# Products made ahead and output rows held back in a graph layer whose edge sums run for most of the kernel

## The chip, the cores and the metric

The kernel runs on one core of a Trainium2 chip. The metric is the device time of one execution in microseconds (us). Three runs of the kernel before took 307.3, 313.0 and 314.23 us, so its median is 313.0 us. One execution was recorded by the hardware profiler; all durations below are of that execution.

The engines are TensorE (PE, with its weight loads shown as PEld), VectorE (DVE), ScalarE (ACT), GpSimd (POOL) and SyncE (SP), which issues most transfers. Each works through its own instructions in order. Transfers run on 16 DMA engines that all queues share.

## The reference

A graph layer over 12,500 nodes of 128 numbers and 412,500 edges of 48 numbers. The edges are sorted by the node they end in (`dst`). `batch0` is all zeros, so one row of the globals serves every node.

```python
h = relu(layernorm(x))
agg = segment_sum(edge_attr, dst, 12500)          # 12500 x 48
z = concat([h, agg, globals[0]]) @ W1 + b1        # 240 -> 256
out = x + relu(z) @ W2 + b2                       # 256 -> 128
```

All of it is in float32.

## The kernel before

**Edge sums.** Edges come in chunks of 896 (seven per partition). A step takes eight chunks, so there are 58 steps (`NS`), of some 217 nodes each. For a step, VectorE builds a one-hot matrix of each edge's place in a window of 32 nodes (`onehot`, L294), TensorE multiplies it with the edges into tile `ps` (`aggregate`), and ScalarE copies the result to `sums` (`keep_sums`, L340). Two steps later TensorE places the sums with a second one-hot (`place_columns`, `place`, tile `pp`), and VectorE adds them (`add`, L371) into `aggT`, which holds the transposed sums: one column per node, 112 of 128 partitions. In a step of TensorE's order the placing of an earlier step comes first, then pieces of the node work, then the aggregation of the step itself. `aggT` is set to zero on POOL in 16 parts of 797 columns (`zero`), each some steps before the sums reach it.

**Node work.** The nodes are in 26 blocks: block 0 has 212 nodes, blocks 1 to 23 have 512, and the last two 256. For a block, in this order: load of its rows (`load_x`, SP, L378), statistics on DVE (`stats`), the root on ACT (`root`), factors on DVE, x + b2 on POOL (`plus_b2`, L411, tile `xb`), normalisation with ReLU on ACT (`normal`, L418, tile `xn`), four transposes on TensorE (`turn`, L182, tile `pt`), a copy out of PSUM (`keep`, L432, tile `hT`), two products with the upper part of W1 into PSUM (`first_h`, tile `ph`), the products with the sums added in the same PSUM tile (`first_a`), bias and ReLU (`relu`, L475), the products with W2 (`second`, tile `po`), the addition of `xb` (`result`, L489, tile `ot`) and the store (`store`, L497, on POOL except for the last two blocks, which SP stores).

**What sets the order.** The order of the whole program is written out. `at(k, f, ...)` puts an operation in half-step `k` (two half-steps to a step). `ready[j]` is the last step whose sums can touch block `j`; `piece` places the turning, the products, and so on of the blocks one after another, where an estimate of TensorE's time per half-step still has room. From that estimate the loop over the steps also chooses how many pairs of edge chunks are multiplied together (`twos`: fewer instructions, more time each).

**Loads.** SP issues the edges of step `s + 3` during step `s`, four transfers of 336 KB a step. `few` lets a load wait until one of the five before it has landed, and in the loop also for the last TensorE instruction that stands before it:

```python
if len(flight) == FLIGHT:
    tc.add_manual_dep(now.ins, flight.pop(0).ins.name, LANDED, reason="few loads under way")
flight.append(now)
if paced:
    tc.add_manual_dep(now.ins, last[0], LANDED, reason="in TensorE's pace")
```

Block rows wait in a pool of five buffers (`xp`), so a load of x also waits until the block five before it has been normalised and added to b2. `xb` has four buffers, so `plus_b2` of a block waits for the result of the block four before it. The weights are eight transfers issued by POOL at the start (`load_weights`). Two extra products of ones (`spare`) stand in half-steps 1 and 3, two more stand before the loop; nothing reads them.

Every matmul goes through one helper line (L178, transposes L182), so tiles tell them apart in the profile. A float32 matmul appears as two records, a transpose as one.

Of the kernel before, what the change touches and what calls it, by code (L numbers as in the profile page):

```python
# [8 lines left out]
F32 = mybir.dt.float32  # L9
I32 = mybir.dt.int32  # L10
AF = mybir.ActivationFunctionType
OP = mybir.AluOpType
# [5 lines left out]
P = 128  # L18
# [4 lines left out]
def kernel(  # L23
# [12 lines left out]
    nc = tc.nc  # L36
    N, D = x.shape
# [59 lines left out]
    ready = [max(s for s in range(NS) if low(s) - BEFORE < a + m * r) for a, m, r in blocks]  # L97


    parts = [(0, 4 * CS)]  # L100
    while parts[-1][0] + parts[-1][1] < NCH:
        c0 = parts[-1][0] + parts[-1][1]
# [38 lines left out]
    with fast:  # L141
# [224 lines left out]
        def add(s):  # L366
            _, v = nc.values_load_multi_w_load_instructions(
                at_i[0:1, s:s + 1], engines=[DVE], min_val=low(s), max_val=high(s),
                skip_runtime_bounds_check_because="clamped to these on the chip")
            to = aggT[:, ds(v[0], WG)]  # L370
            nc.vector.tensor_tensor(to, to, banks_p.pop(s)[:HI + DE, :WG], OP.add)  # L371

        def load_x(j):
            a, m, r = blocks[j]
            xt = xp.tile([P, 4, D], F32, name="xt")
            xv = xt.rearrange("p r d -> p (r d)")[:, :r * D]
            for p0, p1 in by_rows(m):
                now = nc.sync.dma_start(xv[p0:p1], rows_of(x, a + p0 * r, p1 - p0, r))  # L378
            if j > 1:
                few(now)  # L380
            xs[j] = xt

# [24 lines left out]

        def plus_b2(j):
            a, m, r = blocks[j]
            xb = mp.tile([P, 4, D], F32, name="xb", bufs=4)  # L410
# [37 lines left out]
        def first_h(j, h):  # L448
            n, small, ph = bank(j, h)
            product(ph, w1h[:, h * P:(h + 1) * P], ht[j][:, :n], start=(h == 0 or not small),  # L450
                             stop=False, skip_group_check=True)
            hids[j, h] = ph

        def first_a(j):
            a, m, r = blocks[j]
            n = m * r
            for q in range(0, n, 256):
                w = min(256, n - q)  # L460
                for h in range(NH):
                    c = BEFORE + a + q
                    k = slice(0, DE) if bank_is_shared(j) else slice(HI * h, HI * h + DE)
                    product(hids[j, h][:, q:q + w], w1a[k, h * P:(h + 1) * P], aggT[k, c:c + w],
                                     start=False, stop=True, skip_group_check=True)

        def relu(j):
            a, m, r = blocks[j]
# [16 lines left out]

        def result(j):
            a, m, r = blocks[j]
            ot = mp.tile([P, 4, D], F32, name="ot", bufs=3)
            nc.vector.tensor_tensor(ot[:m, :r], pos_o[j][:m, :r], xbs[j][:m, :r], OP.add)  # L489
            outs[j] = ot  # L490

# [6 lines left out]

        def load_weights():
            nc.gpsimd.dma_start(w1h, W1[0:D])  # L500
            nc.gpsimd.dma_start(w1a[0:DE], W1[D:D + DE])
# [56 lines left out]
        with tc.manual_schedule():  # L558
# [14 lines left out]
            ZN = 16  # L573
            zw = -(-aggT.shape[1] // ZN)


            def clear_tail():
                nc.gpsimd.memset(etail, 0.0)
                nc.gpsimd.memset(relt, -1.0)

            def zero(i):
                nc.gpsimd.memset(aggT[:, i * zw:min((i + 1) * zw, aggT.shape[1])], 0.0)

            zero(0)
            nc.vector.memset(eps, EPS)
# [37 lines left out]
            onehot(0)  # L623
            onehot(1)
            load_weights()
# [27 lines left out]
            piece.last = 0  # L653


            def behind(name, j):
                return where[name, j] // 2 * 2 + 2

            def turned(j):
                k = 8 + 3 * j if j < 2 else 2 * placed(ready[j]) - 2  # L660
                piece("turn", j, k, 0.16 * blocks[j][2], (turn, (j,)), (keep, (j,)))

            def hidden_x(j):
                us = 0.22 * blocks[j][2]
                piece("h0", j, behind("turn", j), us, (first_h, (j, 0)))
                piece("h1", j, where["h0", j], us, (first_h, (j, 1)))
# [2 lines left out]
            hidden_x(0)  # L669
            for j in range(NW):  # L670
                r = blocks[j][2]
                piece("a", j, 2 * placed(ready[j]) + (4 if j == 0 else 2), 0.27 * r, (first_a, (j,)), (relu, (j,)))
                if j + 1 < NW:
                    turned(j + 1)
                for q in range(0, r, 2) if j + 1 < NW else ():
                    piece("o", j, behind("a", j), 0.9, (second, (j, q)))
                if j + 1 < NW:
                    hidden_x(j + 1)
                    at(where["o", j] + 1, result, j)
                    at(where["o", j] + 1, store, j)  # L680
# [3 lines left out]
            for j in range(NBL):  # L684
                k = where["turn", j]
                if j > 1:
                    at(k - 17, load_x, j)
                near = j < 2
                at(k - (6 if near else 8), stats, j)
                at(k - (4 if near else 6), root, j)  # L690
# [6 lines left out]
            taken = {where["turn", j] for j in range(NBL)}  # L697

            def apart(k, f, *a):
                while k - 1 in taken or k in taken or k + 1 in taken:  # L700
# [2 lines left out]
                at(k, f, *a)  # L703
                return k

            at(0, shift_dst, 1)
            at(2, spread_dst, 1, 0)
            at(2, spread_dst, 1, 1)
            at(2, middles, 0)
            at(4, own_and_ref, 1)  # L710
            at(6, middles, 1)
# [241 lines left out]
```

## Time and profile before

| | |
|---|---|
| runs | 307.3, 313.0, 314.23 us; median 313.0 |
| profiled execution | 310.81 us, of which 309.1 are its span (first to last instruction) |
| PE busy | 291.4 us (94%) |
| PEld busy | 227.5 us (74%) |
| DVE busy | 231.8 us (75%) |
| ACT busy | 164.1 us (53%) |
| POOL busy | 78.5 us (25%) |
| moved by DMA | 95.15 MB, 308 GB/s over the span |
| granted TensorE clock | 0.994 on average |

The share of the clock is what the throttle granted. The start of an aggregation is the first weight load into `ps` of a step. By the timeline, step 0 begins at 8.76 us, step 1 at 14.97, step 7 at 45.79, step 8 at 51.10, step 15 at 86.24, step 30 at 159.70, step 50 at 258.94 and the last, 57, at 293.24 us. Stretches of idle TensorE say where it waits, and the waits of SP say whether the loads wait for transfers to land or for TensorE.

### The profile page before, as it was taken

The page shows a single profiled execution, that of the slowest core. Times are in us where ns is not written, and L with a number is a line of the kernel's source. Part 1 is how long each engine was busy: PE and PEld are TensorE (multiplying, and loading weights), DVE is VectorE, ACT ScalarE, POOL GpSimd, SP SyncE. Part 2 cuts the span into 40 slices and gives each one's busy share as a digit, 9 for nine tenths or more (in the row PEclk, how much of TensorE's full clock was granted, in tenths as well). Part 3 has the DMA queues.
Part 4 walks back from the last instruction along what each step waited for, and adds up shares of the span by engine and source line. Part 5 has one row for each costly group of instructions (what it writes and reads, how often), then busy time and mean ns, then how long its engine had stood idle before and what let it go on. Part 6 is the DMA issues. An engine that isn't in the chain of part 4 may idle for free. (4 is left out here: it accounts for less than half of the span.)

```text
span 309.1 us, 14799 instructions
## 1 busy us (share of the span) xinstructions
PE 291.4 (94%) x6397; PEld 227.5 (74%) x6398; DVE 231.8 (75%) x530; ACT 164.1 (53%) x426; POOL 78.5 (25%) x87
## 2 busy tenths in 40 slices
PE   7888999999999999989999999999999899999982
PEld 3577767767877877866877887876887777786772
DVE  6867958987695967759976598779984899797221
ACT  2223696465564764645454487655452884665320
POOL 8221041032120544222134204123303033223000
PEclk9997999999999999999999999999999999999999
DMA  7999999999999999999999999999999999998102
GB/s 231 313 322 316 338 338 336 343 361 296 336 344 333 365 349 331 312 333 287 319 354 326 363 335 333 346 348 322 315 367 312 289 354 321 375 357 279 39 0 75
DMA packets 69717, 95.15 MB, mean 308 GB/s; under 512 B 5018, under 2 KB 64611, under 8 KB 69647
## 3 DMA queue, kind: packets, MB, share of 16 engines
q1 hardware_dynamic: 67439, 87.53, 85.3%
q0 software_dynamic: 2208, 6.63, 5.6%
q8 instruction: 51, 0.84, 1.1%
q14 instruction: 19, 0.16, 0.1%
HBM read 87.74 MB, written 6.40 MB: 305 GB/s over the span
## 5 line engine op out<-in xcount | busy, mean ns | idle before, releaser
L178 PE MATMUL ps<-e,oh 128*32 128x48 f32 (+1 forms) x5288 | 117.6, 218 | 7.2 <-issue 4.6
L178 PEld LDWEIGHTS ps<-e,oh 128*32 128x32 f32 (+1 forms) x5288 | 100.7, 116 | 31.4 <-issue 10.2
L294 DVE TENSOR_TENSOR oh<-iota,rel 128x1792 f32<-128x1792 f32 (+1 forms) x60 | 116.0, 1936 | 0.0
L340 ACT COPY sums<-ps 128x192 f32<-128x192 f32 (+1 forms) x165 | 43.1, 262 | 97.5 <-PE ps L178 94.9
L497 POOL DMA_DIRECT2D out_dram<-ot x25 | 14.0, 560 | 207.9 <-DVE ot L489 156.1
L371 DVE TENSOR_TENSOR aggT<-aggT,pp 112x246 f32 x58 | 23.7, 409 | 39.6 <-PE pp L178 30.3
L411 POOL TENSOR_TENSOR xb<-xt,b_sb 128x512 f32<-128x512 f32 (+2 forms) x26 | 46.5, 1792 | 15.3 <-DMA xt<-in_x_dram 9.8
L178 PE MATMUL po<-w,hid 128*128 128x128 f32 (+1 forms) x384 | 47.7, 276 | 1.3 <-ACTq L815 1.3
L178 PE MATMUL ph<-hT,w1h 128*128 128x512 f32 (+2 forms) x100 | 47.5, 578 | 0.6 <-ACT hT L432 0.6
L178 PEld LDWEIGHTS po<-w,hid 128*128 128x128 f32 (+1 forms) x384 | 44.9, 191 | 2.2 <-ACTq L815 1.4
L475 ACT ACTIVATE hid<-ph,bias 128x512 f32<-128x512 f32 (+2 forms) x49 | 30.4, 670 | 24.5 <-PE ph L178 23.3
L418 ACT ACTIVATE xn<-xt,sh,sc 128x128 f32<-128x128 f32 (+1 forms) x98 | 40.5, 483 | 0.5
L178 PE MATMUL pp<-place,sums 128*112 128x128 f32 x232 | 39.7, 295 | 0.0
L178 PEld LDWEIGHTS pp<-place,sums 128*112 128x112 f32 x232 | 29.2, 178 | 7.6 <-issue 1.5
L354 DVE TENSOR_TENSOR place<-iota,pos 128x256 f32<-128x256 f32 x58 | 34.3, 593 | 0.0
L178 PE MATMUL ph<-aggT,w1a 48*128 48x256 f32 (+1 forms) x192 | 28.3, 400 | 0.0
L432 ACT COPY hT<-pt 128x512 f32<-128x512 f32 (+2 forms) x26 | 26.7, 1026 | 3.1 <-PE pt L182 3.1
L489 DVE TENSOR_TENSOR ot<-po,xb 128x512 f32<-128x512 f32 (+2 forms) x25 | 16.6, 665 | 13.5 <-PE po L178 12.2
L178 PEld LDWEIGHTS ph<-aggT,w1a 48*128 48x128 f32 x192 | 17.3, 186 | 10.9 <-issue 7.8
L388 DVE BATCH_NORM_STATS2 st<-xt 128x6 f32<-128x128 f32 (+1 forms) x98 | 21.3, 279 | 1.8 <-DMA xt<-in_x_dram 1.8
L178 PEld LDWEIGHTS ph<-hT,w1h 128*128 128x128 f32 x100 | 16.2, 191 | 6.4 <-issue 3.3
L182 PE MATMUL pt<-ident,xn 128*128 128x128 f32 (+1 forms) x98 | 15.9, 282 | 0.0
(120 smaller groups left out, 139.7 us busy)
## 6 DMA issues: line engine op xcount, KB each, us to landing
e<-in_edge_attr_dram SPq DMA_DIRECT2D x230, 336.0 KB, 5.1
xt<-in_x_dram SPq DMA_DIRECT2D x23, 256.0 KB, 4.8
out_dram<-ot POOLq DMA_DIRECT2D x23, 256.0 KB, 5.5
di<-in_dst_dram SPq DMA_DIRECT2D x3, 448.0 KB, 6.9
xt<-in_x_dram SPq DMA_DIRECT2D x2, 128.0 KB, 4.2
out_dram<-ot SPq DMA_DIRECT2D x2, 128.0 KB, 2.6
di<-in_dst_dram SPq DMA_DIRECT2D x1, 154.0 KB
w1h<-in_L_gnn_W_dram POOLq DMA_DIRECT2D x1, 128.0 KB, 5.6
```

The lines of the kernel that those rows point to most:

```text
L178: last[:] = [nc.tensor.matmul(*a, **k).ins.name]
L182: last[:] = [nc.tensor.transpose(*a, **k).ins.name]
L294: nc.vector.tensor_tensor(to, iota[:, None, :W].to_broadcast([P, n, W]), r[:, :, None].to_broadcast([P, n, W]), OP.is_equal)
L340: nc.scalar.copy(to[k, h], ps[k, h, None, o:o + DE].to_broadcast([k.stop - k.start, h.stop - h.start, 2, DE]))
L354: nc.vector.tensor_tensor(po, iota[:, None, :WP].to_broadcast([P, 2, WP]), pos[:, s, :, None].to_broadcast([P, 2, WP]), OP.is_equal)
L371: nc.vector.tensor_tensor(to, to, banks_p.pop(s)[:HI + DE, :WG], OP.add)
L388: nc.vector.bn_stats(st[:m, q, :], xs[j][:m, q, :])
L411: nc.gpsimd.tensor_tensor(xb[:m, :r], xs[j][:m, :r], b2_sb[:m, None, :].to_broadcast([m, r, D]), OP.add)
L418: nc.scalar.activation(xn[:m, q], xs[j][:m, q], AF.Relu, bias=shift[j][:m, q:q + 1], scale=scale[j][:m, q:q + 1])
L432: nc.scalar.copy(hT[:, :m * r].rearrange("d (p r) -> d r p", r=r), ht[j][:, :m * r].rearrange("d (r p) -> d r p", r=r))
L475: nc.scalar.activation(to, ph, AF.Relu, bias=bias[:, h:h + 1])
L489: nc.vector.tensor_tensor(ot[:m, :r], pos_o[j][:m, :r], xbs[j][:m, :r], OP.add)
```

## The change

Six blocks, 1, 2, 0, 3, 4 and 5 (`FIRST`), have all that does not need the sums done in the first steps: one block a step, from step 0 on. Their rows are loaded straight into columns of `aggT` that no sums reach yet (`kept_x`, from column 3188 on), and b2 is added there in place. Their products with W1 are copied from PSUM into further such columns by ACT (`keep_h`). When the sums of such a block are there, `first_a` starts a new PSUM tile, and DVE adds the kept products to it (`add_h`) ahead of the ReLU. For this `aggT` gets all 128 partitions.

Eight late blocks, 14 to 21 (`HELD`), write their output rows into their own columns of `aggT`, whose sums have been used by then; their stores are put into the last four half-steps. Since POOL runs its instructions in order, they come after the last `plus_b2`.

Four of the loads of x go ahead of the loop along with the edges, the second dst table and its work move by some half-steps, the weights other than W1's upper part are loaded after the aggregation of step 0, and the two `spare` products inside the loop are gone.

```diff
+    FIRST = (1, 2, 0, 3, 4, 5)
+    HELD = range(NBL - 12, NBL - 4)
...
-    aggT = const.tile([HI + DE, N + WG], F32)
+    aggT = const.tile([P, N + WG], F32)
+    kept_x, kept_h = {}, {}
+    c0 = 4 * zw
+    for j in sorted(FIRST):
+        n = blocks[j][1] * blocks[j][2]
+        kept_x[j] = aggT[:, c0:c0 + blocks[j][2] * D].rearrange("p (r d) -> p r d", d=D)
+        c0 += blocks[j][2] * D
+        kept_h[j] = aggT[:, c0:c0 + NH * n].rearrange("p (h n) -> p h n", h=NH)
+        c0 += NH * n
...
-            xt = xp.tile([P, 4, D], F32, name="xt")
+            xt = kept_x[j] if j in FIRST else xp.tile([P, 4, D], F32, name="xt")
...
-            pt = ps_t.tile([P, 512], F32, name="pt")
+            pt = ps_o.tile([P, 512], F32, name="po") if j in FIRST else ps_t.tile([P, 512], F32, name="pt")
...
+        def keep_h(j, h):
+            if bank_is_shared(j):
+                n = blocks[j][1] * blocks[j][2]
+                nc.scalar.copy(kept_h[j], banks[j].rearrange("p (h n) -> p h n", h=NH)[:, :, :n])
+            else:
+                nc.scalar.copy(kept_h[j][:, h], hids[j, h])
+
+        def add_h(j):
...
+                for h in range(NH):
+                    nc.vector.tensor_tensor(hids[j, h], hids[j, h], kept_h[j][:, h], OP.add)
...
+            if j in HELD:
+                ot = aggT[:, BEFORE + a:BEFORE + a + r * D].rearrange("p (r d) -> p r d", d=D)
...
+            load_x(FIRST[0])
             load_step(0)
+            load(1, 0)
+            load(1, 1)
             load_dst(1)
-            load_x(0)
-            load_step(1)
+            load(1, 2)
+            load(1, 3)
+            load_x(FIRST[1])
             load_step(2)
-            load_x(1)
+            load_x(FIRST[2])
+            load_x(FIRST[3])
             for s in range(3, AHEAD):
                 load_step(s)
+            load_x(FIRST[4])
...
+            for i, j in enumerate(FIRST):
+                r = blocks[j][2]
+                if i == len(FIRST) - 1:
+                    at(2, load_x, j)
+                at(2 * i, stats, j)
+                at(2 * i + 1, root, j)
+                at(2 * i + 1, factors, j)
+            for i, j in enumerate(FIRST):
+                at(2 * i + 2, normal, j)
+            for i, j in enumerate(FIRST):
...
+                at(2 * i + 3, turn, j)
+                at(2 * i + 3, keep, j)
+                for h in range(NH):
+                    at(2 * i + 4, first_h, j, h)
+                    if h or not bank_is_shared(j):
+                        at(2 * i + 4, keep_h, j, h)
+                at(2 * i + 5, plus_b2, j)
...
+            for i, j in enumerate(HELD):
+                assert where["o", j] < 2 * NS - 4
+                at(2 * NS - 4 + i // 2, store, j)
...
-            for k in (1, 3):
-                at(k, spare)
```

More of the change, by code (lines that the diff above doesn't have):

```diff
@@ L409, in plus_b2 @@
             a, m, r = blocks[j]
-            xb = mp.tile([P, 4, D], F32, name="xb", bufs=4)
+            xb = xs[j] if j in FIRST else mp.tile([P, 4, D], F32, name="xb", bufs=4)
             nc.gpsimd.tensor_tensor(xb[:m, :r], xs[j][:m, :r], b2_sb[:m, None, :].to_broadcast([m, r, D]), OP.add)
@@ L450, in first_h @@
             product(ph, w1h[:, h * P:(h + 1) * P], ht[j][:, :n], start=(h == 0 or not small),
-                             stop=False, skip_group_check=True)
+                             stop=j in FIRST, skip_group_check=True)
             hids[j, h] = ph
+        def keep_h(j, h):
[5 more added lines that the diff above has]
+        def add_h(j):
+            if bank_is_shared(j):
+                n = blocks[j][1] * blocks[j][2]
+                to = banks[j].rearrange("p (h n) -> p h n", h=NH)[:, :, :n]
+                nc.vector.tensor_tensor(to, to, kept_h[j], OP.add)
+            else:
+                for h in range(NH):
+                    nc.vector.tensor_tensor(hids[j, h], hids[j, h], kept_h[j][:, h], OP.add)
         def first_a(j):
@@ L458, in first_a @@
             n = m * r
+            if j in FIRST:
+                for h in range(NH):
+                    _, small, hids[j, h] = bank(j, h)
             for q in range(0, n, 256):
@@ L461, in first_a @@
                 for h in range(NH):
+                    begin = j in FIRST and q == 0 and (h == 0 or not small)
                     c = BEFORE + a + q
@@ L464, in first_a @@
                     product(hids[j, h][:, q:q + w], w1a[k, h * P:(h + 1) * P], aggT[k, c:c + w],
-                                     start=False, stop=True, skip_group_check=True)
+                                     start=begin, stop=True, skip_group_check=True)
         def relu(j):
@@ L487, in result @@
             a, m, r = blocks[j]
-            ot = mp.tile([P, 4, D], F32, name="ot", bufs=3)
+            if j in HELD:
+                ot = aggT[:, BEFORE + a:BEFORE + a + r * D].rearrange("p (r d) -> p r d", d=D)
+            else:
+                ot = mp.tile([P, 4, D], F32, name="ot", bufs=3)
             nc.vector.tensor_tensor(ot[:m, :r], pos_o[j][:m, :r], xbs[j][:m, :r], OP.add)
@@ L500, in load_weights, with load_weights_of_sums @@
             nc.gpsimd.dma_start(w1h, W1[0:D])
-            nc.gpsimd.dma_start(w1a[0:DE], W1[D:D + DE])
+        def load_weights_of_sums():
+            now = nc.gpsimd.dma_start(w1a[0:DE], W1[D:D + DE])
+            tc.add_manual_dep(now.ins, last[0], LANDED, reason="edges first")
             nc.gpsimd.dma_start(w1a[HI:K2], W1[D:D + DE])
@@ L653 @@
             piece.last = 0
+            for i, j in enumerate(FIRST):
[8 more added lines that the diff above has]
+            for i, j in enumerate(FIRST):
+                r = blocks[j][2]
+                for k, us in ((2 * i + 3, 0.16 * r), (2 * i + 4, 0.44 * r)):
+                    room[k] = room.get(k, SHARE) - us
+                    work[k] = work.get(k, 0.0) + us
+                at(2 * i + 3, turn, j)
+                at(2 * i + 3, keep, j)
+                for h in range(NH):
+                    at(2 * i + 4, first_h, j, h)
+                    if h or not bank_is_shared(j):
+                        at(2 * i + 4, keep_h, j, h)
+                at(2 * i + 5, plus_b2, j)
             def behind(name, j):
@@ L659, in turned @@
             def turned(j):
[L660 removed]
+                if j in FIRST:
+                    return
+                k = 2 * placed(ready[j]) - 2
                 piece("turn", j, k, 0.16 * blocks[j][2], (turn, (j,)), (keep, (j,)))
             def hidden_x(j):
+                if j in FIRST:
+                    return
                 us = 0.22 * blocks[j][2]
@@ L679 @@
                     at(where["o", j] + 1, result, j)
-                    at(where["o", j] + 1, store, j)
+                    if j not in HELD:
+                        at(where["o", j] + 1, store, j)
             for j in (NBL - 2, NBL - 1):
@@ L684 @@
             for j in range(NBL):
+                if j in FIRST:
+                    continue
                 k = where["turn", j]
[L686 to L690, printed above, removed]
+                at(k - 17, load_x, j)
+                at(k - 8, stats, j)
+                at(k - 6, root, j)
                 at(k - 4, factors, j)
@@ L694 @@
             at(where["a", 0] - 2, bias_of_globals)
-            taken = {where["turn", j] for j in range(NBL)}
+            for i, j in enumerate(HELD):
+                assert where["o", j] < 2 * NS - 4
+                at(2 * NS - 4 + i // 2, store, j)
+            taken = {where["turn", j] for j in range(NBL) if j not in FIRST}
             def apart(k, f, *a):
```

24 lines of the change are left out of this document (13 added, 11 removed).

## The prediction

> **What bounds the kernel now.** I read the stretches of 10 us first, then the waits, then the timeline, for the starts of the aggregations (matmul weight loads into tile ps) and for durations. Columns of the first view: stretch and its length, busy time of each engine with the number of instructions, granted TensorE clock, DMA share, GB/s.
>
> ```profile
> 0.00:10.00 10.00, 8.00 (x81) 3.80 (x84) 7.26 (x25) 2.11 (x5) 7.58 (x20) 1.00 0.80 246
> 10.00:20.00 10.00, 8.02 (x183) 6.03 (x179) 7.00 (x19) 2.84 (x9) 0.89 (x1) 1.00 1.01 316
> 20.00:30.00 10.00, 8.25 (x136) 7.14 (x136) 7.37 (x31) 3.09 (x12) 3.24 (x3) 0.83 0.98 320
> 30.00:40.00 10.00, 8.85 (x202) 7.40 (x202) 9.09 (x21) 7.02 (x20) 0.00 (x0) 1.00 1.01 339
> 40.00:50.00 10.00, 10.00 (x223) 7.72 (x224) 6.83 (x18) 9.68 (x27) 3.82 (x4) 1.00 1.02 330
> ...
> 130.00:140.00 10.00, 9.09 (x187) 7.00 (x174) 5.56 (x8) 3.97 (x10) 3.32 (x3) 1.00 0.93 312
> ...
> 290.00:300.00 10.00, 10.00 (x225) 8.29 (x224) 2.31 (x6) 2.71 (x7) 0.00 (x0) 1.00 0.06 23
> ```
>
> TensorE idles 6.9 us in the first 40 us, and after that hardly at all; the DMA engines are full from the start to about 283 us and nearly empty after. So in the middle both are full, and neither alone is worth much. Who yields to whom is in the waits (time, times, longest):
>
> ```profile
> SPq L127 <- DMA e<-in_edge_attr_dram: 116.4, 179, 3.0
> ...
> SPq L127 <- PE pp L178: 5.7, 20, 0.4
> ...
> SPq L378 <- ACT hid L475: 2.0, 1, 2.0
> ...
> PEld ps L178 <- DMA e<-in_edge_attr_dram: 4.6, 8, 0.8
> ...
> POOL out_dram L497 <- DVE ot L489: 156.1, 17, 13.7
> ```
>
> SyncE mostly waits for the landing of one of its own five loads under way, seldom for TensorE's pace. By the trace's landings, the last edges of a step arrive 1.2 us before its aggregation ends in step 1, 2.9 in step 6, 3.4 in step 24, again 1.2 in step 30 (ends at 162.0 us), 5.1 in step 50. About 1.2 us is the least possible, since the last chunks are used last. So edges bind up to step 5 and once more at steps 25 to 30; elsewhere TensorE binds, with 2 to 5 us of slack behind it.
>
> **The change, part by part.** The rows that price it:
>
> ```profile
> 13.00 0.60 ACT L252 COPY rel<-pt 128x512 f32<-128x512 f32 x1 [1.26 <-PE pt L182]
> ...
> 13.92 1.13 PE L178 MATMUL ph<-iota,ones 128*128 128x512 f32 x2
> ...
> 163.07 1.65 ACT L418 ACTIVATE xn<-xt,sh,sc 128x128 f32<-128x128 f32 x4
> ...
> 164.63 0.69 DVE L489 TENSOR_TENSOR ot<-po,xb 128x512 f32<-128x512 f32 x1 [1.37 <-PE po L178]
> ...
> 168.14 1.02 PE L178 MATMUL ph<-hT,w1h 128*128 128x512 f32 x2
> ...
> 170.16 0.66 PE L182 MATMUL pt<-ident,xn 128*128 128x128 f32 x4
> ```
>
> *Products made early (TensorE).* A full block costs 0.66 us of transposes and 2 x 1.02 of products, 2.7 us; five of these and the small block (about 1.2) are 14.7 us. Blocks 0 and 1 and part of 2 and 3 stood in steps 4 to 8 already. I priced each step's TensorE instructions in the built order of both programs by rows like these: at the end of step 7 the new kernel has done 6.8 us more, at step 15 1.7 us less (the two fillers of 1.13 that it drops), and from step 22 on the steps are alike. So work moves from steps 8 to 15 into steps 2 to 7, where the idle time is; nothing after step 22 gets lighter.
>
> *What it adds.* Per full block two copies of 512 columns out of PSUM on ScalarE (no such copy in the trace; between 0.60, the row above, and 1.11, the mean of the transposed copy L432; I take 0.61, as both sides are contiguous): 1.2 us. And two additions on VectorE, by the 0.69 of L489 1.4 us, 7 us in all. Of these additions, none is on the path in steps 7 to 15: VectorE then has one-hots 2.02, place 0.59, add 0.41 and 0.9 a step for additions and results, 4 us of the 4.9 that a step takes. Behind a waiting addition stand place and the one-hot of two steps on; ReLU waits for it, and the second products one step later: 1.4 + 0.69 of work in about 2.6 us of aggregation and place. Uncovered it would be up to 2 us a block, 12 us; inside the stretch that waits for edges I take 0.
>
> *Loads.* Blocks 1, 2, 0, 3, 4 are asked for before the loop, block 5 in step 1. Before, block 4 was issued at 34.0 and block 5 at 43.2 us, so two loads of 256 KB come early. By the trace's packet records one load is 128 packets of 2 KB, 93 ns each, over 16 engines: 0.74 us, 1.5 us in all for the edges behind them in SP's queue. Against it the eight weight loads on POOL, which share the engines in 6 to 12 us, mostly go behind step 0. I take 0 (bounds -1 and +1.5). The early loads need no x buffer, and the next five find theirs free: in SP's queue the waits for buffers go up to block 10 (2.0 us at 124.8 us is the largest seen).
>
> *Stores.* Eight late stores leave steps 38 to 55. A store is 64 packets of 4 KB at 168 ns, 0.67 us of all engines, 5.4 us in all. But TensorE binds there. The 10 us rows from 200 to 290 us show it idle for 2.1 us, and that is the most that this can be worth; below nothing I see no way. I take 1.5. At the end POOL meets them after the last b2 addition, whose buffer waits for the result of block 21, near step 54. Eight stores of 0.67 and issues of 0.56 are about 5.4 us beginning near 282 us, in a DMA share of 0.06; the last result comes at 304. Cost 0; uncovered, if they ran behind the last result, 5 us.
>
> *Steps 0 to 30, the main term.* The idle time filled is 6.8 us, but the bytes ahead of step 30 are the same, so the clock there is set by how fast the edges come. If they came as before, step 30 would end at 162.0 again: gain 0. If they follow, because SP's waits for TensorE's pace go (8.3 us between 43 and 162 us) and buffer waits (9.4 us at the x loads, partly the ordinary wait for a landing), the gain is the banked work: 6.8 + 1.7 less copies and fillers' loss, about 7. Five loads are in flight, so a late issue costs the queue only a part: 8.3 / 5 = 1.7, and for the buffers about 1.3. I take **3.0**, nearer the lower end, since 116 us of SP's waits are for landings.
>
> *The sum*, on the profiled execution of 310.8 us (span 309.1 and 1.7 around it): 310.8 - 3.0 - 1.5 = 306.3. The median of the runs is 313.0, 2.2 above that execution, so I forecast **308.5 us**. A change of about 2% (6.3 us) is what a measurement here can tell from none.
>
> *The clock.* After the sparse stretch of 18 to 26 us the granted clock was 0.51 from 25.7 to 29.2 us, which is why the third row above says 0.83. A further such window costs 1.75 us of work. Dropping two fillers thins steps 0 and 1, so one or two windows may be added there: 1.75 to 3.5 us out of the banked 6.8, which changes the point at which the second rival decides and not the sum. The Trainium skill (TensorE: Matmul & The Clock Gate, Part 1) says that the gate opens after about 3.4 us of sustained work and closes after an idle window as long; the trace agrees in the length of the window, 3.4 us. By that rule alone the change would start cold and lose up to the whole 3.5.
>
> **The rivals.**
> 1. *The edges follow TensorE.* Then 7 us come out of steps 0 to 30 and 2 later: 310.8 - 9 = 301.8, on the median's scale 304. For it: bytes per us reach 360 between 260 and 280 us, where buffers and pace rarely stop SP, against 334 between 86 and 162. Against it: the many waits for landings. Chance 0.33.
> 2. *The early steps get serial (slower).* In steps 1 to 6 ScalarE has per step sums 0.82, root 0.29, normalisation 1.93, transposed copy 1.11, kept copies 1.22: 5.4 us, VectorE 5.2, both in order, where a step took 5.1 us (14.97 to 45.79 us for steps 1 to 7). If normalisation, transposes, copy, products and kept copies (1.93 + 0.66 + 1.11 + 2.04 + 1.22 = 6.96) and the sums 0.82 run one after another, a step takes 7.8, 16 us more by step 7. It decides from the point where the delay passes the banked 6.8 us, 1.1 us a step; at full size it costs 9.4: 320 on this execution, 322 on the median's scale. Against it: the calls of one block are spread over three steps. Chance 0.14.
> 3. *The edges alone bind.* Step 30 stays at 162.0 and TensorE after it as before; at most the stores' relief remains: 310.8 - 0.8 = 310, median's scale 312. So the early products would do nothing. Chance 0.18.
>
> **How the numbers follow.** Forecast 0.35, rivals 0.33, 0.14 and 0.18. Faster by over 2% (under 306.7) is rival 1 and a little of the forecast: 0.37. Slower by over 2% (above 319.3) is most of rival 2: 0.11. Within 2%: 0.52. The range takes in rivals 1 and 3 with the runs' own spread (307.3 to 314.2) and the mild part of rival 2: 301 to 315.
>
> **What would show it.** In the new profile, TensorE busy above 9 of 10 us from 10 us on, and ScalarE at 8 or more up to 50 us; step 7 ending near 47 us; step 15 beginning at 84 to 86 us; step 30 ending at 158 to 160; if it ends below 156, rival 1 is right, at 162 rival 3. DMA in the slices after 283 us should rise from 0.06 to about 0.4 with the end unmoved against the last result. If step 8 begins after 58 us (51.1 before), rival 2 has come. The forecast fails if landings speed up or slow down by themselves: 1% of 285 us of DMA is nearly 3 us.

## The result, and the profile after

The changed kernel took **326.56 us** (median of four runs, 322.68 to 328.87); the kernel before 310.83 (four runs, 307.3 to 314.23). The ratio is **1.052, with a 95% interval of 1.036 to 1.069**: slower, outside the range on record (301 to 315), on the side of the second rival, to which the prediction gave 0.14. Ratios in this document compare undisturbed executions alone, while the times given are medians of all. The fourth run of the kernel before took 308.66 us, so its median comes down from the 313.0 of the first three runs to 310.83, about the profiled execution.

The profiled execution took 325.99 us, 324.2 of them its span, against 310.81 and 309.1. The whole loss is made in the first 74 us. Starts of the aggregations, from the timeline:

| step | 0 | 1 | 4 | 6 | 8 | 15 | 30 | 57 | end |
|---|---|---|---|---|---|---|---|---|---|
| before | 8.76 | 14.97 | 29.96 | 41.80 | 51.10 | 86.24 | 159.70 | 293.24 | 309.1 |
| after | 7.15 | 18.82 | 40.65 | 62.37 | 74.03 | 102.82 | 176.46 | 307.91 | 324.2 |
| later by | -1.6 | 3.9 | 10.7 | 20.6 | **22.9** | 16.6 | 16.8 | 14.7 | 15.1 |

Up to step 8 the kernel falls 22.9 us behind; from step 8 to 15 it takes 28.8 us instead of 35.1 and gets 6.3 back, which is the work done early; then it runs level and gains another 1.5 by the end. 22.9 - 6.3 - 1.5 = 15.1.

The stretches of 10 us of the changed kernel (columns as before: stretch, length, busy time of PE, PEld, DVE, ACT, POOL with instructions, granted TensorE clock, DMA share, GB/s):

```profile
0.00:10.00 10.00, 7.97 (x93) 4.46 (x95) 7.31 (x25) 2.10 (x5) 3.81 (x13) 1.00 0.83 276
10.00:20.00 10.00, 3.23 (x74) 2.66 (x70) 7.64 (x32) 3.98 (x10) 0.80 (x2) 0.77 0.99 328
20.00:30.00 10.00, 9.62 (x150) 7.48 (x142) 4.87 (x12) 6.79 (x18) 3.29 (x6) 0.89 0.99 270
30.00:40.00 10.00, 6.81 (x113) 4.80 (x111) 8.62 (x30) 6.29 (x16) 5.80 (x5) 0.97 1.02 341
40.00:50.00 10.00, 10.00 (x200) 7.97 (x199) 3.90 (x12) 5.31 (x12) 1.27 (x1) 0.69 0.68 202
50.00:60.00 10.00, 4.54 (x34) 2.08 (x21) 5.71 (x8) 9.73 (x28) 0.00 (x0) 0.99 0.51 149
60.00:70.00 10.00, 9.55 (x135) 6.82 (x135) 1.07 (x3) 2.30 (x6) 3.04 (x4) 0.67 0.47 121
...
130.00:140.00 10.00, 10.00 (x228) 8.03 (x224) 8.50 (x18) 5.00 (x14) 3.47 (x3) 1.00 0.99 320
...
290.00:300.00 10.00, 10.00 (x270) 7.82 (x270) 6.67 (x13) 4.98 (x15) 1.76 (x3) 1.00 0.76 260
```

Two things are new, and they take turns. In 10 to 20, 30 to 40 and 50 to 60 us TensorE stands idle (3.23, 6.81, 4.54 of 10 busy). In the stretch or half stretch behind each, the granted clock is down (0.77 and 0.89, 0.69, 0.67): the records show three windows at half rate, 15.42 to 22.24, 39.31 to 46.14 and 59.79 to 66.62 us, 6.83 us each. Before there was one, of 3.41. The DMA share falls from 40 us on (0.68, 0.51, 0.47): the edges are now far ahead and wait for TensorE, as SyncE's waits say (time, times, longest; before, the line for PE po had 3.3 us):

```profile
SPq L144 <- DMA e<-in_edge_attr_dram: 113.3, 171, 2.4
...
SPq L144 <- PE ps L195: 13.7, 19, 3.3
...
SPq L144 <- PE po L195: 12.9, 11, 7.7
```

What TensorE waits for stands in the timeline (start, duration, engine, line, operation, tiles, size; in brackets the idle time before and what ended it). L195 is the matmul helper, L199 the transposes, L449 the copy `hT`, L276 part of `check_dst`:

```profile
10.85 0.19 PE L195 MATMUL po<-perm,first 32*1 32x4 f32 x2
11.81 2.02 DVE L311 TENSOR_TENSOR oh<-iota,rel 128x1792 f32<-128x1792 f32 x1
12.22 1.65 ACT L435 ACTIVATE xn<-aggT,sh,sc 128x128 f32<-128x128 f32 x4
15.61 0.87 DVE L405 BATCH_NORM_STATS2 st<-aggT 128x6 f32<-128x128 f32 x4 [1.78 <-DMA aggT<-in_x_dram]
16.84 0.69 DVE L215 TENSOR_SCALAR df<-di,first 128x896 f32<-128x896 int32 x1
17.52 0.14 DVE L256 TENSOR_TENSOR dev<-po,cen 1x4 f32<-1x4 f32 x1
17.80 1.09 PE L199 MATMUL po<-ident,xn 128*128 128x128 f32 x4 [6.77 <-DVE dev L256]
...
35.37 1.48 PE L199 MATMUL po<-ident,xn 128*128 128x128 f32 x4
38.41 0.30 ACT L414 ACTIVATE sc<-mv,eps 128x4 f32<-128x4 f32 x1 [1.41 <-DVE mv L407]
38.62 1.04 ACT L449 COPY hT<-po 128x512 f32<-128x512 f32 x1
39.72 1.01 PE L195 MATMUL po<-u,w1u 64*128 64x1 f32 x4 [2.86 <-ACT hT L449]
...
54.31 1.48 PE L199 MATMUL po<-ident,xn 128*128 128x128 f32 x4
57.48 1.04 ACT L276 ACTIVATE sc<-df,over 128x896 f32<-128x896 f32 x1
59.32 1.03 ACT L449 COPY hT<-po 128x512 f32<-128x512 f32 x1
60.40 2.04 PE L195 MATMUL po<-w,hid 128*106 128x128 f32 x8 [4.61 <-ACT hT L449]
```

The three long ones are waits for the tile `po`, of which there is one buffer. At 11 us it holds the result of `middles(0)`, ready at 11.04. Its reader on VectorE (`dev`, L256) comes at 17.52, since ahead of it in VectorE's order stand a one-hot, the statistics of the second early block, which wait for that block's rows, and the second dst table. The normalised rows (L435) had been there since 13.9. At 37 and at 56 us `po` holds an early block's transposes, and what stands next in TensorE's order is another user of `po`: `bias_of_globals`, and the second products of block 0. The copy that frees the tile stands in ScalarE's order behind a root that waits for VectorE, and behind `check_dst(1)`, 3 us long. A fourth stop, 1.06 us at 51 us, is for the same copy behind `check_dst(0)`.

Idle time of TensorE up to the start of step 8 is 18.2 us, before 6.8. So of the 22.9 us, 11.4 are idle time. The rest is the time that TensorE's records take: 14 more records of products with W1 +6.6, 12 more transposes +3.4, the fillers -2.7, and +4.2 for the other work, above all aggregations (+1.4) and second products (+1.1) that fall into the half-rate windows.

### The profile page after: what moved, and what is told of

Same layout as the page of the kernel before. It is cut to its first block, busy times and chain, and to the rows that moved or that the text cites. A ratio compares the mean times of both kernels' runs of the same rounds, so it can differ in the third digit from the quotient of the medians.

```text
span 324.2 us, 14746 instructions
## 1 busy us (share of the span) xinstructions
PE 296.4 (91%) x6373; PEld 232.8 (72%) x6374; DVE 235.6 (73%) x541; ACT 169.1 (52%) x437; POOL 73.8 (23%) x87
## 5 line engine op out<-in xcount | busy, mean ns | idle before, releaser
L195 PE MATMUL ps<-e,oh 128*32 128x48 f32 (+1 forms) x5268 | 119.8, 222 | 3.5 <-issue 3.4
L195 PEld LDWEIGHTS ps<-e,oh 128*32 128x32 f32 (+1 forms) x5268 | 103.8, 120 | 25.6 <-issue 7.0
L195 PE MATMUL po<-w,hid 128*128 128x128 f32 (+1 forms) x384 | 48.7, 280 | 5.9 <-ACT hT L449 4.6
L195 PEld LDWEIGHTS po<-w,hid 128*128 128x128 f32 (+1 forms) x384 | 45.6, 194 | 7.0 <-ACT hT L449 4.8
L428 POOL TENSOR_TENSOR xb<-xt,b_sb 128x512 f32<-128x512 f32 (+1 forms) x20 | 34.3, 1717 | 68.3 <-DVE aggT L530 49.4
L195 PE MATMUL ph<-hT,w1h 128*128 128x512 f32 (+2 forms) x100 | 48.0, 584 | 1.1 <-ACT hT L449 1.1
L538 POOL DMA_DIRECT2D out_dram<-ot x17 | 9.4, 553 | 142.5 <-DVE ot L530 114.6
L195 PE MATMUL pp<-place,sums 128*112 128x128 f32 x232 | 40.3, 298 | 0.0
L195 PEld LDWEIGHTS pp<-place,sums 128*112 128x112 f32 x232 | 29.5, 180 | 7.7 <-issue 1.5
L435 ACT ACTIVATE xn<-xt,sh,sc 128x128 f32<-128x128 f32 x76 | 31.4, 483 | 0.4
L195 PE MATMUL ph<-aggT,w1a 48*128 48x256 f32 (+1 forms) x192 | 29.1, 401 | 0.0
L371 DVE TENSOR_TENSOR place<-iota,pos 128x256 f32<-128x256 f32 x58 | 28.3, 489 | 0.0
L195 PEld LDWEIGHTS ph<-aggT,w1a 48*128 48x128 f32 x192 | 17.7, 186 | 10.7 <-issue 7.0
L195 PEld LDWEIGHTS ph<-hT,w1h 128*128 128x128 f32 x100 | 16.8, 196 | 7.6 <-issue 4.2
L449 ACT COPY hT<-pt 128x512 f32<-128x512 f32 (+1 forms) x20 | 20.7, 1033 | 1.5 <-PE pt L199 1.5
L405 DVE BATCH_NORM_STATS2 st<-xt 128x6 f32<-128x128 f32 x76 | 16.5, 278 | 0.0
L530 DVE TENSOR_TENSOR ot<-po,xb 128x512 f32<-128x512 f32 (+1 forms) x11 | 7.3, 664 | 9.4 <-PE po L195 8.0
L414 ACT ACTIVATE sc<-mv,eps 128x4 f32<-128x4 f32 (+2 forms) x26 | 7.6, 293 | 10.2 <-DVE mv L407 7.2
```

What stands on the lines that cost most here:

```text
L195: last[:] = [nc.tensor.matmul(*a, **k).ins.name]
L371: nc.vector.tensor_tensor(po, iota[:, None, :WP].to_broadcast([P, 2, WP]), pos[:, s, :, None].to_broadcast([P, 2, WP]), OP.is_equal)
L405: nc.vector.bn_stats(st[:m, q, :], xs[j][:m, q, :])
L414: nc.scalar.activation(sc[:m, :r], mv[:m, :r, 1], AF.Sqrt, bias=eps[:m])
L435: nc.scalar.activation(xn[:m, q], xs[j][:m, q], AF.Relu, bias=shift[j][:m, q:q + 1], scale=scale[j][:m, q:q + 1])
L449: nc.scalar.copy(hT[:, :m * r].rearrange("d (p r) -> d r p", r=r), ht[j][:, :m * r].rearrange("d (r p) -> d r p", r=r))
```

## The experiments

**Theory**: the loss comes from the early transposes' tile. They were put into `po`, which `middles`, `bias_of_globals` and the second products use too, and each user stands behind the last one's reader, wherever that is in its engine's order; the half-rate windows follow from the idle stretches. **Rivals**: A, ScalarE's order is too long whatever the tile (the predicted rival 2 in another form); B, the clock itself, through the two missing fillers; C, the held stores.

**1. The other tile.**

```diff
-            pt = ps_t.tile([P, 512], F32, name="pt") if i else ps_o.tile([P, 512], F32, name="po")
+            pt = ps_t.tile([P, 512], F32, name="pt") if i > 1 else ps_o.tile([P, 512], F32, name="po")
...
-            pt = ps_o.tile([P, 512], F32, name="po") if j in FIRST else ps_t.tile([P, 512], F32, name="pt")
+            pt = ps_t.tile([P, 512], F32, name="pt")
```

> The transposes of the six early blocks go into the pool of tile pt again, and the middles of parts 0 and 1 into po; nothing is left out. Theory (the early transposes share the single tile po with middles, bias_of_globals and the second products, and stand behind its slow readers): the stall of 6.8 us at 11 us falls to 2 to 3 us, those of 2.9 at 37 us and 4.6 at 56 us mostly go, of the three half-rate windows at most one or two are left, step 8 begins at 56 to 64 us instead of 74.0, and the time is 305 to 316 us. Rival A (ScalarE's queue itself is too long, whatever the tile): the transposes wait as long for another reader, step 8 begins after 70 us, 322 to 327 us. Rival B (the clock, through the missing fillers): the half-rate windows stay, 322 us or more.

Measured: 313.28 us against 310.75 beside it, ratio 1.011 (1.003 to 1.019). Step 8 begins at 60.28 us. No half-rate window before 300 us. These are all the idle stretches of 0.7 us or more that are left between 8 and 80 us:

```profile
19.87 0.69 PE L195 MATMUL pp<-place,sums 128*112 128x128 f32 x4 [0.96 <-DVE place L371]
...
44.40 1.98 PE L195 MATMUL ph<-hT,w1h 128*128 128x512 f32 x4 [1.21 <-ACT hT L449]
...
52.52 1.99 PE L195 MATMUL ph<-hT,w1h 128*128 128x512 f32 x4 [1.57 <-ACT hT L449]
```

Two tile assignments changed give back 13 of the 16 us, with the same operations in the same order on every engine. The theory holds, and rivals A and B fall as explanations of the whole. What is left of A are the two waits for `hT`, 2.8 us.

**2. ScalarE's order alone.**

```diff
-            at(10, check_dst, 0)
-            at(12, check_dst, 1)
+            at(17, check_dst, 0)
+            at(19, check_dst, 1)
```

> Only check_dst of parts 0 and 1 (about 3 us of ScalarE each) is moved from half-steps 10 and 12 to 17 and 19; nothing is left out. Theory of the tile po: the stalls of 6.8 and 2.9 us stay, those of 1.2 and 4.6 us, where ScalarE's copy out of po stood behind check_dst, go, and with them the window at 60 us: 4 to 8 us less, 318 to 322 us. Rival A (ScalarE's load, not the tile): the work comes a few us later and the stalls with it, within 2 us of the changed kernel. Rival B (the clock alone): stalls smaller but three windows as before, 1 to 3 us less.

Measured: 315.24 us (two runs), ratio to the kernel before 1.014 (1.007 to 1.021); 11 us less than the changed kernel, more than expected. What TensorE still waits for:

```profile
17.98 1.09 PE L199 MATMUL po<-ident,xn 128*128 128x128 f32 x4 [6.58 <-DVE dev L256]
...
39.08 0.60 PE L195 MATMUL po<-u,w1u 64*128 64x1 f32 x4 [2.27 <-ACT hT L449]
...
53.60 1.12 PE L195 MATMUL po<-w,hid 128*106 128x128 f32 x8 [1.73 <-ACT hT L449]
```

The first two waits stay, as expected. The third falls from 4.61 to 1.73 and the one at 52 us goes. The half-rate window behind them is gone and the one at 40 us is down to 3.41 us, while the first has grown to 10.24 (12.71 to 22.95 us): 13.7 us in all instead of 20.5. So a tile's price is the position of its reader: with `check_dst` out of the way the shared tile costs much less. Experiments 1 and 2 cut the same waits from two sides, and their gains do not add.

**3. Fillers into the idle stretches.** Ten products of ones, whose results nobody reads:

```diff
+            fill(3, turn, 5)
+            fill(where["a", 0] - 2, bias_of_globals, 2)
+            fill(where["o", 0], second, 3)
```

> The changed kernel with ten filler products more, whose results nobody reads, ahead of the three instructions at which TensorE stood still (five before the transposes of block 1, two before bias_of_globals, three before the first second products). Theory (waits for po, and the clock as their consequence): the stalls' ends stay where they are, the half-rate windows at 15, 39 and 60 us go or get shorter, about 5 us less, 320 to 323 us, still far above the kernel before. Rival B (the clock is the cause): nearly all of the loss goes, under 315 us. If fillers cannot fill a wait, because the processing is late anyway: 326 to 330 us.

Measured: 319.52 us (two runs; ratio to the kernel before 1.028, 1.020 to 1.036), 7.0 less than the changed kernel. Where the stretch of 10 to 20 us had a clock of 0.77, it now has 1.00, and there is no half-rate window in the first 300 us:

```profile
11.99 4.56 PE L195 MATMUL ph<-iota,ones 128*128 128x512 f32 x10
17.89 0.63 PE L199 MATMUL po<-ident,xn 128*128 128x128 f32 x4 [1.34 <-DVE dev L256]
```

The first stop ends where it did (17.89 against 17.80 us). The later ones end 1.1 to 3.3 us sooner, the clock's gain piling up. So the clock costs some **7 us** of the 15.7 us loss by the medians, 5.5 by the two profiled executions. It is a consequence: the fillers, some 9 us, cover the waits but leave them in place, and with them 8.8 us of loss.

**4. Without the held stores.**

```diff
-    HELD = range(NBL - 12, NBL - 4)
+    HELD = range(0)
```

> The changed kernel without the held stores: every output row leaves behind its result as before. Theory: the loss is all in the early blocks, so 0 to 2 us more than the changed kernel, step 8 begins at 73 to 75 us. Rival C (the stores piled up at the end cost): 3 to 5 us less, and the last instruction comes earlier after step 57.

Measured: 329.42 us (two runs), ratio 1.059 (1.052 to 1.067); step 8 begins at 72.88. Rival C falls: the stores held back do not cost. By the medians they save 2.9 us here, a difference that lies within the two intervals.

**5. Experiments 1 and 2 together.**

> The edits of the first and the second experiment together: the early transposes in pt, middles of parts 0 and 1 in po, check_dst of parts 0 and 1 at half-steps 17 and 19; nothing is left out. The first experiment still had stalls of 1.2 and 1.6 us where the products waited for ScalarE's copy behind check_dst. Theory (TensorE binds from step 8 on, so what it stands still before comes out at the end): these 2.8 us go, step 8 begins near 57.5 us, the span is 305 to 307 us and the time 307 to 310 us by the runs of the first experiment (313.3), below or level with the kernel before. Rival (the edges bind there, or other waits take their place): no change against the first experiment, 312 to 314 us.

Measured: median 309.76 us of eleven runs against 312.14 of the kernel before, 2.4 us less; the ratio, which rests on four of the eleven, is 0.984 (0.977 to 0.992). The same kernel in a second series (experiment 11): 309.32 against 311.62, 2.3 us less, ratio 0.994 (0.989 to 0.999). So with its waits mended the change comes out **0.6 to 1.6% faster** than the kernel before. The first interval reaches 2.3% and the second ends near nothing, so it isn't settled whether the change is worth the 2% that count as faster here; by the medians it is worth 0.7 to 0.8%. Step 8 begins at 56.97 and 56.29 us in the two profiles; both waits for `hT` are gone. In the first of the two, what is left up to step 8 is this:

```profile
12.77 1.63 PE L199 MATMUL pt<-ident,xn 128*128 128x128 f32 x4 [1.27 <-ACT xn L435]
...
19.41 0.69 PE L195 MATMUL pp<-place,sums 128*112 128x128 f32 x4 [1.95 <-DVE place L371]
```

Each of the two waits is followed by a half-rate window of 3.41 us. In the second profile they are 1.65 and 1.63 us, with one window of 6.83 us that begins after the first and lasts past the second.

**6. The held stores in the kernel before**, without the early products (the diff is the one in the section on the change, for `HELD` alone).

> The kernel before with the eight held stores alone, no early products; nothing is left out. The prediction gave the stores 1.5 us, at most 2.1: 308.5 to 311 us where the kernel before has about 310.8. Rival (fewer DMA packets beside the edges in steps 38 to 55 let the edges come sooner): 3 us or more less. Rival (the piled-up stores reach past the last result): up to 5 us more.

Measured: 310.13 us against 312.14, eleven runs, ratio 0.994 (0.990 to 0.998). That is 2.0 us by the medians, where the prediction had 1.5 and at most 2.1. By the medians the stores thus make 2.0 of the 2.4 and 2.3 us that experiments 5 and 11 gain; by the ratios they make 0.6% of 1.6%, or all of 0.6%. What the early products themselves are worth without their waits lies between nothing and one per cent.

**7. Only the first holder of `po` changed.**

```diff
-            pt = ps_t.tile([P, 512], F32, name="pt") if i else ps_o.tile([P, 512], F32, name="po")
+            pt = ps_t.tile([P, 512], F32, name="pt")
```

> The changed kernel with one word undone: middles of part 0 write pt instead of po, so that the early transposes, still in po, no longer stand behind their readers on VectorE; nothing is left out. Theory (each stall has its own holder of po): the stall of 6.8 us at 11 us falls to under 2 us and its half-rate window goes, the stalls at 37, 50 and 56 us stay: 7 to 10 us less than the changed kernel, 316 to 320 us. Rival (the wait only moves, since the transposes need VectorE's statistics anyway): within 3 us of the changed kernel.

Measured: 322.36 us (two runs, beside a kernel before at 312.14; ratio 1.033, 1.021 to 1.045). The waits are as expected:

```profile
13.86 1.48 PE L199 MATMUL po<-ident,xn 128*128 128x128 f32 x4 [0.75 <-ACT xn L435]
...
34.89 0.60 PE L195 MATMUL po<-u,w1u 64*128 64x1 f32 x4 [1.70 <-ACT hT L449]
...
54.30 2.04 PE L195 MATMUL po<-w,hid 128*106 128x128 f32 x8 [4.61 <-ACT hT L449]
```

The 6.77 us became 0.75, and the normalised rows are now what ends the wait; the other two are there. But the gain is 4 us of time (5.5 if each kernel is taken against the kernel before beside it), not 7 to 10. At step 8 the kernel is 6.2 us ahead of the changed one (67.79 us); at step 57 it is 4.5. Windows at half rate came all the same, at 15.86, 36.34 and 53.41 us, 13.7 us in all instead of 20.5. So the wait did go, and its price was overrated, in part by what comes back later: between 84 and 310 us TensorE waits 1.7 us for edges, in the changed kernel 0.2 at most (experiment 8 has more of this).

**8. Fillers on top of experiment 5**: one before the first transposes, two before the first placement.

```diff
+            todo[3][i:i] = [(quiet, ())]
...
                 if s == 1:
+                    quiet()
+                    quiet()
                     place_columns(0)
```

> The fifth experiment's kernel with three filler products of 1.1 us whose results nobody reads: one before the transposes of block 1 (idle 1.26 us there), two before the first placement (idle 1.95 us). The computation is whole. Theory of the clock (an idle stretch of 1 to 2 us is followed by half rate): the slow window of 3.4 to 6.8 us between 14 and 24 us goes, step 8 begins 2 to 3.5 us before 57.0, and the time is 1 to 3 us under that of the fifth experiment in the same call. Rival (the window comes whatever TensorE does): the fillers cost up to 1 us.

Measured: median 309.95 us of five runs (305.09 to 315.42) against 311.62, ratio 0.988 (0.978 to 0.998; it rests on two of the five): no better than experiment 5. The profile, of an execution of 311.88 us, the second longest of the five, has no half-rate window in the first 300 us, and step 8 begins at 55.90 and step 15 at 84.19 us, 2.0 ahead of the kernel before. At step 57 it is 0.7 *behind* it. Its waits between 84 and 295 us say where the lead went; in the kernel before the like lines hold 0.2 us in all:

```profile
PEld ps L195 <- DMA e<-in_edge_attr_dram: 2.5, 3, 1.8
PE ps L195 <- DMA e<-in_edge_attr_dram: 2.1, 3, 1.7
```

(The two lines show the same idle time, once for the weight loads and once for the products.) By the landings of the trace, the last edges arrive 1.2 to 1.5 us before the end of the aggregation in steps 15, 27, 29 and 30, about the least that any of these traces shows; in the kernel before only step 30 is at that mark. In this execution TensorE has caught up with the edges, and what was won early is taken back. It isn't so in every execution of the mended kernel. In the profile of experiment 5 (307.28 us) the lead over the kernel before grows from 0.7 us at step 15 to 3.7 at step 57, without a wait of TensorE for edges in the same view. In that of experiment 11 (311.09 us) it shrinks from 1.5 to 0.2, with waits of 0.5 us.

**9. The later blocks one step later**, so that VectorE does not wait for rows ahead of the first placement (experiment 5 plus this):

```diff
+                late = 2 * (i > 0)
-                at(2 * i, stats, j)
+                at(2 * i + late, stats, j)
```

and likewise for root, factors, normalisation, turning, products and b2.

> The fifth experiment's kernel with statistics, normalisation, transposes and products of the five early blocks after the first one step later each, so that VectorE does not wait for block 2's x load (2.25 us) ahead of the first placement; nothing is left out. Theory: the stall of 1.95 us at 19.4 us goes and with it a slow window, step 8 begins 1 to 4 us before 57.0, time 1 to 4 us under that of the fifth experiment. Rival (the later blocks now crowd steps 3 to 8 on ScalarE): new stalls of 1 us or more after 35 us, no gain or up to 3 us more.

Measured: 311.60 us against 311.62 (eleven runs), ratio 1.003 (0.999 to 1.007). The stall at 19.4 us and the half-rate windows are gone, and step 5 begins at 37.82 instead of 41.79 us. But step 8 begins at 58.07. The longest idle stretch left, 2.48 us at 52.7 us, lies inside a placement, and the profile names nothing that it waited for (its word for that is `issue`):

```profile
55.17 0.36 PE L195 MATMUL pp<-place,sums 128*112 128x128 f32 x1 [2.48 <-issue]
```

The rival's outcome, then, though by a pause whose cause is open.

**10. The shared tile in the kernel before.**

```diff
-            pt = ps_t.tile([P, 512], F32, name="pt")
+            pt = ps_o.tile([P, 512], F32, name="po") if j < 6 else ps_t.tile([P, 512], F32, name="pt")
```

> The kernel before with the transposes of its first six blocks in po instead of pt, and nothing else; nothing is left out. Theory (sharing po costs only where its holder waits behind a loaded ScalarE or VectorE; in the kernel before the second products come 2 us or more after the transposes): 0 to 3 us more, stalls of 1 us or less. Rival (the shared tile costs its several us wherever it is): 5 us or more.

Measured: 314.04 us against 311.62 (nine runs), ratio 1.009 (1.004 to 1.013). The cost is 2.4 us, by waits like these (ScalarE's copy behind a `check_dst` that ends at 38.84 us):

```profile
38.66 0.18 ACT L259 ACTIVATION_READ_ACCUMULATOR sc<-pos,overp 128x1 f32 x1
38.75 1.03 ACT L432 COPY hT<-po 128x512 f32<-128x512 f32 x1
...
39.84 1.12 PE L178 MATMUL po<-w,hid 128*106 128x128 f32 x8 [1.47 <-ACT hT L432]
```

So the tile alone has a price of some 2.4 us (1 to 4 by the interval), with single waits of 1.1 to 1.5 us. In the crowded first steps of the changed kernel the same sharing went with 11 us more of idle time.

**11. Experiment 5 again**, beside 8 and 9.

> The fifth experiment's kernel once more, beside the two that are built on it: 306 to 311 us, 1 to 4 us under the kernel before.

Measured: the 309.32 us given under 5.

## Why the prediction was wrong

**The step that failed** is in the part on the early products. It priced the transposes at 0.66 us a block and the products at 2.04 as work that moves into idle time, and the diff's other word in `turn`, `po` for `pt`, at nothing: it is not in the working at all. A tile with one buffer belongs to an engine's order as much as the operation does. The sum needed a term for each user of `po` after another: 6.8, 2.9 and 4.6 us. Who waits behind whom can be read from the orders: for the first, that `dev` stands behind a one-hot and behind statistics that wait for rows; for the last, that `hT` stands behind 3 us of `check_dst`. The sizes follow from them only in part, since how late the rows land stands in no order. The prediction asked what stands behind a waiting addition on VectorE. It did not ask what stands ahead of a tile's reader.

**Rival 2** named the side and, nearly, the size (322 us; a step of 7.8 us against the 7.9 measured from step 1 to 8). That the numbers agree is luck, since its mechanism is not what happened. It took normalisation, transposes, copy, products and kept copies of a block for a serial chain. Experiment 1 leaves that chain as it is, and a step takes 6.5 us there. Of the 9.2 us by which it is late at step 8, 8.0 are TensorE's time for the work done early (products +6.4, transposes +4.3, fillers -2.7). Some 2.8 us of that are transposes waiting for their quarters of the normalisation, the one piece of the chain that shows (below). The remaining 1.2 us are all that is left for the rest of it, so the chain costs at most about 4 us and not the 16 to which the rival added it up. Its point of decision was right: step 8 after 58 us.

**The clock** was mis-sized: one or two windows of 3.4 us were allowed for, 1.75 to 3.5 us, blamed on the fillers. There were three of 6.83, worth 7 us (experiment 3). The cause was right only in part: the windows follow the waits, and they are gone in experiment 1, which has no fillers before these places either. The shorter waits of experiment 5 still bring 6.8 us of windows, and the profile with three fillers there has none (experiment 8). Nor does the clock only move the point at which the second rival decides, as the prediction had it: it is between a third and a half of the loss. The Trainium skill (TensorE: Matmul & The Clock Gate, Part 1, on HAM oscillation) describes a loop in which each wait is followed by a cold start; here its price is the 5.5 to 7 of the 15.7 us.

**The banked work** was right in kind and somewhat too large. From 6.8 us more at the end of step 7 to 1.7 less at step 15, the forecast made the steps between 8.5 us lighter; they are 6.3 lighter. By the records of these steps, products and transposes take 7.5 us less (none is left, against 6.02 and 1.46 before), but the aggregations take 1.1 more (14.53 us in 588 records, against 13.38 in 657), since the loop over the steps multiplies more pairs of edge chunks together where it sees room. That early transposes cost more was missed: they take each quarter of the normalisation as it comes, 1.48 us a block instead of 0.66 (22 transposes take 5.72 us in experiment 1 against 2.82 before).

**The main term**, 3.0 us for edges that partly follow TensorE, could not show in the changed kernel, whose edges land 2.3 us or more ahead of need in every step from 1 on that the landings show. In the mended kernels it can. The profile of experiment 8 is 2.0 us ahead at step 15 and has nothing left at step 57, with TensorE waiting for edges that land at the last moment. That is rival 3, "the edges alone bind", in that execution; the one of experiment 5 keeps its lead. How much of the 3.0 could be had stays open: the profiles of experiments 5, 11 and 8, all with step 8 near 56 to 57 us, reach step 57 at 289.6, 293.0 and 293.9 us. (The slack of 5.1 us that the prediction read for step 50 is a misreading: the last edges land at 257.32 us and the aggregation ends at 260.8, which makes 3.5 at most.)

**The stores**: 1.5 us forecast, 2.0 measured (experiment 6). (The third rival counted the same stores with 0.8 and gave no reason.) Their issue at the end costs nothing that shows, as forecast: six go out in one piece 13 us before the last store on POOL.

```profile
303.96 3.19 POOL L538 DMA_DIRECT2D out_dram<-aggT  x6
317.48 0.54 POOL L538 DMA_DIRECT2D out_dram<-ot  x1 [10.32 <-DVE ot L530]
```

**Additions and kept copies**: sized rightly (0.69 us as forecast, and 0.59 against 0.61). No idle time of TensorE ends with an addition in the changed kernel's waits. **The loads of x**: the edges did not come late, but the rows did. VectorE waits 1.78 us for the second block's, and in its order the reader of `po` is behind that.

Of what was to show the steps right, TensorE above 9 of 10 from 10 us on and ScalarE at 8 up to 50 us failed at once (3.23 and 3.98 in the second stretch).

## What to carry to other kernels

When an operation gets another PSUM tile, write down for each buffer its users in TensorE's order, and for each the reader that frees it and what stands ahead of that reader in its engine's order; a free slot in TensorE's time is of no use while the tile is held elsewhere. Count an idle stretch of TensorE more than once over: in this kernel 11 us of waits cost another 5.5 to 7 us of clock, and fillers remove the second part but not the first. And before work is moved into an early gap, ask what binds later: here the mended version loses its lead to the edges in two of its three profiles (experiments 11 and 8).

## What the hardware showed unasked

Half rate needed less idle time than expected. The windows are 3.41 us long or multiples of it. In the second experiment the clock fell at 12.71 us, when TensorE had stood idle for 1.3 us, behind an aggregation of step 0 with gaps for edges; in the seventh a window began at 36.34 us, behind 1.70 us of idle time and 1.48 us of transposes that wait for their quarters. The Trainium skill (TensorE: Matmul & The Clock Gate, Part 1) puts the closing after at least one idle window of about 3.4 us; these two stretches hold no full one, so the trace differs. Its Part 4 says that transposes do not count as busy in the same way. That explains neither: in the second experiment no transposes stand there, and in the seventh only some 0.3 us of them lie in the 3.41 us before the fall, beside the 1.70 us of idle time. Nor does the idle time alone decide: in the third experiment TensorE stood idle for 2.09 us before 38.65 us, and no window followed. The same kernel can differ from one execution to the next: the two profiles of experiment 5's kernel have their windows at different times.
